# A decoder layer on one core: row maxima written straight into the queries' rows, and a shorter planned distance between attention and output projection

## The chip, the cores and the metric

The kernel runs on one core of a Trainium2 chip. The metric is device time in microseconds (us) of one execution. Engine names are those of the profile: PE is TensorE (PEld its weight loads), DVE VectorE, ACT ScalarE, POOL GpSimd, SP SyncE. SP computes nothing; it issues most DMA transfers, in the order of its program, and a transfer that has to wait for a semaphore holds up everything behind it on SP.

## What is computed

The input x has 16 batches of 128 positions and 1024 channels, and there is a context of the same shape. Cut to what matters here:

```python
# attention: groups of 128 rows are independent; 32 query heads, 8 key heads, head size 32
q, k = rope(x_ln @ Wq), rope(x_ln @ Wk); v = x_ln @ Wv
scores = q @ k.T / sqrt(32), causal
x = x + softmax(scores) @ v @ Wo
# autocorrelation with the context: correlations per channel by Fourier transform,
# the 9 largest delays per channel, softmax over them, weighted sum of delayed values
x = x + autocorrelation(layernorm(x), context)
# four mixed streams: 24 logits per position; a 4x4 matrix by 50 Sinkhorn iterations
# mixes the streams, and one 256x256 branch is added
```

All is float32. The matrix products of the projections run as sums of exact parts (high and low), so that each of them is three products.

## The kernel before, in words

**Two parts.** The first part (lines 182 to 318) projects four batches at a time into rotated queries, keys and values, transforms the context into spectra, and leaves all of it in DRAM (`qd`, `kd`, `vd`, `sd`). Two of the sixteen batches' spectra are left over for the beginning of the second part. The second part (from line 320) takes the batches one by one through attention, output projection, autocorrelation, and mixed streams.

**One batch in the second part** is the generator `batch` (line 775). Its stages, in order:

- `keys` and `queries` (lines 396 and 404) load the keys (`ks`) and, for each half f of the heads (sixteen heads), a tile `qs` of 98 rows. Rows 0 to 95 hold the parts of the queries. Rows 96 and 97 are to hold the negated row maxima, in a high and a low part; the keys' tile has ones there, so that the product of scores (line 447) subtracts the maximum by itself. There are two buffers of `qs`, which is one batch's worth.
- `maxima` (line 412) computes the scores once (line 421), takes the maxima of each row (DVE, line 428) into a tile of [128 positions, 16 heads], transposes it on PE (line 432), and splits the negated result on ACT into `nh` (line 434) and on DVE into `nl` (line 436), both [16 heads, 128 positions]. Then SP writes both to a small DRAM tensor (line 438, two transfers of 8 KB, 32 times two in all) and reads them back as two rows of 2048 values into `qs[96:98]` (line 439, one transfer of 16 KB).
- `attended` (line 441) computes the scores again with the maximum subtracted (line 447), their exponential (ACT, line 451), the causal cut (POOL, line 452), the sums and the values' sums on PE (lines 460 and 464), the division (lines 467 to 476) and its split into `ch` and `cl` (lines 492 and 494). `ch` and `cl` have two buffers each, again one batch's worth; `ch` of the next batch can be written only when the output projection of this one has read it.
- `projected_out` (line 502) is 24 matmuls for each half of the channels (lines 507 to 509), added to `xt` on DVE (line 500). `xt` is loaded just before (line 793, 512 KB).
- Then come the layer norm (`qn`, lines 162 and 169), `delays` (line 528) and `delayed` (line 565). Both call `cross` (line 513), which loads a spectrum of 512 KB into `sv` (line 518; six a batch, two buffers) and multiplies with it on DVE (line 523) and POOL (lines 524 and 525).
- `logits` (line 588) stores `xt` and the normed `z` (lines 590 and 593) and ends in the 24 logits (line 615); `branch` (line 618) ends in an accumulating store that POOL issues (line 657).
- After the last batch of each of three groups (0 to 6, 7 to 12, 13 to 15), `sinkhorn` (line 666) runs 49 iterations of small operations on DVE and POOL, and `mixed` (line 723) mixes the streams of each batch of the group (lines 731 to 766).

**What sets the order.** Each generator yields planned distances in us (`T_...`, lines 36 to 39 and 48), and the loop at line 828 always advances the flow that is due first. A new batch is due every `PERIOD` = 33. That gives the order in which the program is written down, and so the priority of each instruction. The framework then orders every engine's instructions by that priority among those which its own timing model holds to be ready, and inserts the semaphores. So the planned distances are priorities and not times, and an instruction whose buffer is not free is passed by others of lower priority.

**Planned places.** Counted from the due time of its batch, the yields put the first scores of attention at 19.8 and its last sums at 32.9, the output projection at 87.7 and 92.8, the layer norm at 97.9, the store of z at 147.1, the end of the branch at 189.1. The first Sinkhorn blocks of the three groups are due at 387.1, 585.1 and 684.1. The two spectra that are left over are due at 39.7 and 64.2; the first call of `q_late` (line 327, in the output projection of batch 0 at 87.7) would emit what is left of them.

Of the kernel before, what the change touches and what calls it, by code (L numbers as in the profile page):

```python
# [11 lines left out]
FP = mybir.dt.float32  # L12
FR = mybir.dt.float32r
# [7 lines left out]
B, L, D = 16, 128, 1024  # batches, positions, channels  # L21
NK = D // 128  # chunks of 128 channels
HD, NH, NKV = 32, 32, 8  # attention: head size, query heads, key heads
TG = 4  # batches that share one projection
# [3 lines left out]
TOPK = 9  # int(2 * ln(128))  # L28
# [5 lines left out]
# The order of the program: us between batches, and between the parts of one.  # L34
PERIOD = 33
T_S, T_MX, T_M, T_ST, T_PT, T_SUM, T_DIV, T_OUT = 0, 3.29, 13.22, 1.0, 2.56, 54.8, 422239.83, 5.08
T_LN, T_X, T_DEL, T_TOP, T_WT, T_X2, T_DLD = 7.24, 5, 0, 9.35, 3.53, 2.3, 1.0
T_Z, T_ZT, T_LT, T_LOG, T_XP, T_XPT = 15, 2.82, 0.76, 8.03, 14.22, 1.18
SKS, MIXS = [45.0, 257.52, 400.81, 8, 8, 8], [11.22, 56.61, 24.78, 4, 4, 4]
# [8 lines left out]
T_FILL, T_SPEC = 39.7, 24.48  # L48
# [5 lines left out]
# The constant matrices, each [128, 128], in the order in which they lie in the input "mats".  # L54
# [4 lines left out]
def constant_matrices():  # L59
    """Rope tables, causal mask, and the real Fourier matrices of 128 positions.  # L60

    Rows 0..63 of a spectrum are real parts and rows 64..127 imaginary ones. At the even
    frequencies (k / 128) row 0 is frequency 0 and row 64 is frequency 64, both real; the odd ones
    are (k + 1/2) / 128. With a spectrum V of the context and one Q of the other sequence,
    V[re, re] * Q + V[im, im] * [Q im, -Q re] holds the real parts of a cross spectrum and, below
    them, its imaginary parts; at row 0 and 64 of the even frequencies V[im, im] is zero and
    V[re, re] has the real value.

    Frequency 0 adds the same to every correlation of a channel. Neither their order nor their
    softmax depends on it, so that "g" leaves it out, and "f_c" can add to frequency 0 the 128 of  # L70
    the last value by which the even half of the delayed sums lacks half the last value.
    """
    m = {}
    inv = (1.0 / np.float32(500000.0) ** (np.arange(0, HD, 2, dtype=np.float32) / np.float32(HD))).astype(np.float32)
    freqs = (np.arange(L, dtype=np.float32)[:, None] * inv[None]).astype(np.float32)
    m["cos"] = np.repeat(np.cos(freqs).T, 8, 0)
    m["sin"] = np.repeat(np.sin(freqs).T, 8, 0)
    p = np.arange(128)
    m["mask"] = np.where(p[None] > p[:, None], NEG, 0.0)
    m["ident"] = np.eye(128)  # L80
    t, f = np.arange(128)[:, None], np.arange(64)[None]
    sign = (-1.0) ** t
    even = 2 * np.pi * ((t * f) % 128) / 128
    odd = 2 * np.pi * ((t * (2 * f + 1)) % 256) / 256
    im = -np.sin(even)
    im[:, :1] = sign
    m["f_k"] = np.concatenate([np.cos(even), im], 1)
    m["f_c"] = m["f_k"].copy()
    m["f_c"][127, 0] += 128
    m["f_w"] = np.concatenate([np.cos(odd), -np.sin(odd)], 1)  # L90
    # Of the values less the last one.
    m["f_u"] = m["f_w"].copy()
    m["f_u"][127] -= m["f_w"].sum(0)
    g = np.concatenate([np.cos(even), -np.sin(even)], 1).T * 2 / 128
    g[0], g[64] = 0, sign[:, 0] / 128
    m["g"] = g
    ge = np.concatenate([np.cos(even), np.sin(even)], 1).T / 128
    ge[0], ge[64] = 1 / 256, sign[:, 0] / 256
    m["ge"] = ge
    m["go"] = np.concatenate([np.cos(odd), np.sin(odd)], 1).T / 128  # L100
    # Row 32 s + i to column i.
    m["sel"] = (p[:, None] % 32 == p[None]) * 1.0
    return np.ascontiguousarray(np.stack([m[k] for k in FIRST + SECOND], 1).astype(np.float32))


def constant_tokens():
    """Of row 4 t + j, one in column t."""
    return np.repeat(np.eye(32, dtype=np.float32), 4, 0)
# [3 lines left out]
def tile_decoder(ctx: ExitStack, tc, x, cx, wqkv, wo, wlog, base, gate, wb, mats, toks, zero, eye4, out):  # L112
# [3 lines left out]

    SPQ = (SP, ACT)[SQ]
# [6 lines left out]
    # What the first part leaves to the second: rotated queries and keys in two exact parts each,  # L124
    # values, and the context's spectra (even re, even im, odd re, odd im; each twice, below each other).
# [5 lines left out]
    def rsqrt(v, eps):  # L131
        """1 / sqrt(v + eps), with a Newton step behind the tables."""
# [13 lines left out]
    def layernorm(o, i):  # L146
        """Into o; the variance and the factor too."""
        st = small.tile([128, 2, 6], FP, name="st")
        for n in range(2):
            DVE.bn_stats(st[:, n, :], i[:, n * 512 : (n + 1) * 512])  # L150
        mv = small.tile([128, 2], FP, name="mv")
        DVE.bn_aggr(mv, st)
        r = rsqrt(mv[:, 1:2], LN_EPS)
        DVE.tensor_scalar(o, i, mv[:, 0:1], r, ALU.subtract, ALU.mult)
        return mv[:, 1:2], r

    def layernorm_act(o, i, sums, norm):
        """The same on ScalarE, of the sums of two halves."""
# [13 lines left out]
    def over(a, n):  # L172
        """[128, m] -> [128, m, n]"""
        return a.unsqueeze(2).to_broadcast([128, a.shape[1], n])

    def repeat(a, n):
        """[128, m] -> [128, n, m]"""
        return a.unsqueeze(1).to_broadcast([128, n, a.shape[1]])

# [1 line left out]
    # The last spectra fill the beginning of the second part: what they need lies to the right.  # L181
# [3 lines left out]
    with ExitStack() as att:  # L185
# [12 lines left out]
        def weights(j, n):  # L198
            """A block of 256 columns, half of its rows."""
# [39 lines left out]
        def rotated(xh, xl, col, d):  # L239
            """Two chunks of features, of the first and the second halves of eight heads."""  # L240
# [38 lines left out]
        def tokens(g):  # L279
            """Begun before the projections of the group before it are done."""  # L280
# [14 lines left out]
        # Keys, values, then queries.  # L295
# [31 lines left out]
    def q_late():  # L327
        """What the first batch needs behind the last spectra."""
# [36 lines left out]
    # The ninth largest, and no others.  # L365
# [15 lines left out]
    # sigmoid(gate), and (1 - sigmoid(gate)) on the diagonal.  # L381
# [12 lines left out]
    max_d = [[dram.tile([2, 16, 128], FP, name=f"mx{b}_{f}") for f in range(2)] for b in range(B)]  # L394
# [17 lines left out]
    def maxima(b, ks, qs, f):  # L412
        """Of the masked scores of sixteen heads, negated, in two parts into the rows 96 and 97."""
# [19 lines left out]
        nh = q2.tile([16, 128], FR, name="nh")  # L433
        ACT.activation(nh, tp, AF.Copy, scale=-1.0)
        nl = q2.tile([16, 128], FR, name="nl")
        DVE.scalar_tensor_tensor(nl, tp, -1.0, nh.bitcast(FP), ALU.mult, ALU.subtract)
        for i, o in enumerate((nh, nl)):
            SP.dma_start(out=max_d[b][f][i], in_=o.bitcast(FP))
        SP.dma_start(out=qs[96:98, :].bitcast(FP), in_=max_d[b][f].rearrange("i h t -> i (h t)"))

    def attended(b, ks, qs, v, f):
        """Sums over the values of the keys of sixteen heads, and the sums of the weights."""
# [22 lines left out]
        # The reciprocal of the sums, which lie on the rows of the values already.  # L465
# [4 lines left out]
        # A Newton step behind the tables.  # L470
# [26 lines left out]
    def added(xt, n, ps, sums, sign=1.0):  # L497
        """The half n of xt, and its sum."""
# [14 lines left out]
    def cross(b, i, of, m, cols):  # L513
        """Cross spectrum of the context with `of`, [128 positions, 512 channels]."""
# [13 lines left out]
    def delays(b, qn, cols):  # L528
        """Weights of the delays of 512 channels, zero but for the largest."""
# [7 lines left out]
        # The nine largest of each channel become -BIG in `kept`.  # L537
# [27 lines left out]
    def delayed(b, xt, cols, kept, sums):  # L565
        """out[l] = sum of w[tau] v[min(l + tau, 127)]"""
# [21 lines left out]
    def logits(b, xt, lg, sums):  # L588
# [5 lines left out]
        # The mean of z ** 2.  # L594
# [23 lines left out]
    def branch(b, xt, z, lg):  # L618
        # Softmax of the two sets of four.
# [46 lines left out]
    def sinkhorn(Z, n, gi):  # L666
        """exp(Z + u + v) of the last iteration, [128, n, 4, 4]; Z is of that shape too.

        The first iteration runs in logarithms, less the maximum. Behind it every sum over a row or
        a column is within 1/16 and 4 for any Z: the other direction was normalised just before, so  # L670
        that it holds an element of 1/4 at least, divided by a sum of 4 at most. REFRESH iterations
        then scale exp(Z + u + v) itself, and u and v follow from the products of their sums. What
        exp underflows to zero would grow by 16 ** (2 * REFRESH) at most until logarithms take over
        again: to less than 1e-21.
        """
# [3 lines left out]
        # Negated: u, then v.  # L679
# [43 lines left out]
    def mixed(bs, lg):  # L723
        """The mixed streams of some batches, in parts."""
# [10 lines left out]
        # Row (t, j) of 32 positions to row (t, i).  # L735
# [39 lines left out]
    def batch(b):  # L775
        """In parts; each yields the time until the next, as the order of the program has it."""
# [104 lines left out]
```

## Time and profile before

| | |
|---|---|
| times of three runs, us | 1389.58 (the median), 1391.62, 1378.53 |
| span of the profiled execution, first to last instruction, us | 1391.9 |
| its busy time, share of the span: PE, DVE, POOL, ACT | 81%, 63%, 48%, 42% |
| granted TensorE clock, mean of the profile | 0.891 |
| first part of the program | until about 400 us |
| first and last scores of attention (line 447), us | 430.9 and 1104.4 |
| first and last addition of the output projection (line 500), us | 459.9 and 1136.8 |
| last branch (line 657), us | 1223.1 |
| streams mixed (line 761), us | 1228.7 to 1383.0 |

The profiled execution's own time lies in its span of 1391.9 us, which is 0.3 us above the longest of the three runs and 2.3 us above their median. Lines of the profile name an instruction by its line in the kernel, its engine, and what it writes and reads (`qs<-mx` reads the DRAM tensor of the maxima into `qs`). In the lists of waits, the columns are the total idle time in us, how often, and the longest. "SPq" is SP's queue of transfers: such a line says what SP waited for before it could issue.

### The profile page before, as it was taken

Reading aid. Unit: us, or ns where it says so; the run is one execution under the profiler, and the core shown is the slowest. Engines: PE = TensorE matmul, PEld = TensorE weight load, DVE = VectorE, ACT = ScalarE, POOL = GpSimd, SP = SyncE. Lnnn points to the kernel's source line nnn. Section 1 sums busy time; section 2 is a strip of 40 time slices with the busy share of each in tenths; the row PEclk is TensorE's granted clock in tenths of the full one; section 3 lists DMA queues with packets and bytes.
Section 4 is the critical chain, followed back from the end, with each engine's and each line's share of the span. In section 5 each row is a group of like instructions: output and inputs, shape, how many; then the busy total and the mean of one; then the engine's idle time right before and its main releaser. Section 6 shows DMA issues by size and latency. Waiting matters only on the chain.

```text
span 1391.9 us, 17636 instructions
## 1 busy us (share of the span) xinstructions
PE 1134.1 (81%) x5024; PEld 725.9 (52%) x5024; DVE 874.0 (63%) x2910; ACT 580.5 (42%) x1281; POOL 673.0 (48%) x813
## 2 busy tenths in 40 slices
PE   5999969989847999999999998999998976452232
PEld 3888748758623555645565555645564553231121
DVE  5463332321123466977788778968897999986840
ACT  3331221221223355557565666556555755321010
POOL 0353313223413365565566656676766766643332
PEclk9999989989956999999999999999999987655555
DMA  6662864765898444576556664476455444365265
GB/s 227 213 215 84 229 204 123 229 196 137 245 271 250 123 129 140 156 200 166 152 161 170 194 180 135 131 183 156 145 158 153 123 119 115 87 121 106 49 121 76
DMA packets 141824, 221.78 MB, mean 159 GB/s; under 512 B 23264, under 2 KB 86112, under 8 KB 141664
## 3 DMA queue, kind: packets, MB, share of 16 engines
q1 hardware_dynamic: 127936, 199.99, 49.1%
q0 software_dynamic: 10752, 16.78, 8.4%
q10 hardware_dynamic: 3040, 3.90, 0.9%
q8 instruction: 39, 0.64, 0.2%
q14 instruction: 57, 0.47, 0.1%
HBM read 129.93 MB, written 90.83 MB: 159 GB/s over the span
## 4 chain that ended last, share of the span: by engine, by line
PE 40%; DVE 27%; DMA 16%; issue 6%; ACT 4%; SPq 4%; POOL 3%; POOLq 0%; DVEq 0%; ACTq 0%
PE mm L249 4%; PE mm L247 4%; PE mm L248 4%; PE sm L460 4%; PE av L464 3%; PE ps L516 3%; DMA sv<-sd 3%; DMA out<-mx 2%; DVE mx L428 2%; PE o L507 2%; DVE kept L542 2%; DMA sd<-F 2%; PE ps L227 2%; PE o L508 2%; DVE P L523 2%
## 5 line engine op out<-in xcount | busy, mean ns | idle before, releaser
L524 POOL TENSOR_TENSOR s<-s,sv 128x512 f32<-128x512 f32 x96 | 125.2, 1305 | 64.6 <-ACT s L521 47.3
L753 PE MATMUL ps<-mz,hm 128*128 128x256 f32 x128 | 59.4, 622 | 97.5 <-POOL hm L745 71.9
L525 POOL TENSOR_TENSOR P<-P,s 128x512 f32<-128x512 f32 x96 | 125.9, 1313 | 13.3 <-DVE P L523 11.6
L247 PE MATMUL mm<-xh,wh 128*128 128x512 f32 x320 | 131.2, 412 | 0.0
L248 PE MATMUL mm<-xl,wh 128*128 128x512 f32 x320 | 126.6, 396 | 0.2 <-DVE xl L216 0.2
L249 PE MATMUL mm<-xh,wl 128*128 128x512 f32 x320 | 125.5, 392 | 0.0
L257 POOL TENSOR_TENSOR ra<-ra,rb 128x512 f32<-128x512 f32 x40 | 50.4, 1279 | 155.3 <-DVE rb L256 155.2
L507 PE MATMUL o<-woh,ch 128*128 128x512 f32 x256 | 108.9, 425 | 8.3 <-DVE xt L500 6.1
L452 POOL TENSOR_SCALAR_AFFINE_SELECT pt<-pt 128x512 f32<-128x512 f32 x128 | 83.7, 668 | 64.7 <-ACT pt L451 63.0
L508 PE MATMUL o<-woh,cl 128*128 128x512 f32 x256 | 106.8, 417 | 4.7 <-POOL cl L494 4.7
L421 PE MATMUL sc<-ks,qs 96*128 96x128 f32 x512 | 98.2, 323 | 10.1 <-DMA qs<-qd 10.1
L228 ACT COPY F<-ps 128x512 f32<-128x512 f32 x64 | 36.5, 585 | 158.5 <-DMA sd<-F 85.5
L509 PE MATMUL o<-wol,ch 128*128 128x512 f32 x256 | 101.9, 398 | 0.0
L428 DVE TENSOR_REDUCE mx<-sc 128x4 f32<-128x512 f32 x128 | 86.4, 680 | 23.7 <-PE sc L421 23.7
L421 PEld LDWEIGHTS sc<-ks,qs 96*128 96x128 f32 x512 | 82.4, 204 | 33.0 <-issue 26.6
L753 PEld LDWEIGHTS ps<-mz,hm 128*128 128x128 f32 x128 | 36.0, 305 | 120.7 <-POOL hm L745 82.0
L523 DVE TENSOR_TENSOR P<-sv,ps 128x512 f32<-128x512 f32 x96 | 64.8, 675 | 52.6 <-ACT s L521 38.1
L227 PE MATMUL ps<-raw,am 128*128 128x512 f32 x128 | 71.1, 681 | 30.6 <-ACT F L228 25.7
L451 ACT ACTIVATE pt<-sc 128x512 f32<-128x512 f32 x128 | 73.7, 598 | 31.5 <-PE sc L447 30.5
L460 PE MATMUL sm<-pt,ones 128*32 128x512 f32 x256 | 79.7, 617 | 1.9 <-POOL pt L452 1.9
L520 ACT COPY s<-ps 64x512 f32<-64x512 f32 x96 | 56.0, 583 | 55.9 <-PE ps L516 40.2
L516 PE MATMUL ps<-wT,bm 128*128 128x512 f32 x128 | 70.8, 638 | 9.3 <-ACT wT L571 8.9
(171 smaller groups left out, 2852.3 us busy)
## 6 DMA issues: line engine op xcount, KB each, us to landing
sv<-sd SPq DMA_DIRECT2D x96, 512.0 KB
qs<-qd SPq DMA_DIRECT2D x96, 256.0 KB
sd<-F SPq DMA_DIRECT2D x80, 256.0 KB
xt<-in_x SPq DMA_DIRECT2D x32, 512.0 KB
out<-mx POOLq DMA_DIRECT2D x32, 512.0 KB, 5.9
sd<-F SPq DMA_DIRECT2D x48, 252.0 KB
raw<-in_cx SPq DMA_DIRECT2D x16, 512.0 KB
qd<-hi SPq DMA_DIRECT2D x32, 256.0 KB
```

What stands on the lines that cost most here:

```text
L247: PE.matmul(ps, lhsT=wh[:, k, c], rhs=h, start=k == 0, stop=False)
L248: PE.matmul(ps, lhsT=wh[:, k, c], rhs=r, start=False, stop=False)
L249: PE.matmul(ps, lhsT=wl[:, k, c], rhs=h, start=False, stop=k == NK - 1)
L421: PE.matmul(sc[:, j, :], lhsT=qs[0:96, h * 128 : (h + 1) * 128], rhs=ks[0:96, g * 128 : (g + 1) * 128], start=False, stop=j == 3,)
L428: DVE.tensor_reduce(mx[:, 4 * s : 4 * s + 4], sc, AX.X, ALU.max)
L460: PE.matmul(sm[32 * s : 32 * s + 32, :], lhsT=ones, rhs=pt, start=True, stop=True)
L507: PE.matmul(ps, lhsT=h, rhs=woh[:, k, cols], start=k == 0, stop=False)
L508: PE.matmul(ps, lhsT=r, rhs=woh[:, k, cols], start=False, stop=False)
L509: PE.matmul(ps, lhsT=h, rhs=wol[:, k, cols], start=False, stop=k == NK - 1)
L516: PE.matmul(ps, lhsT=M[m], rhs=of, start=True, stop=True)
L524: POOL.tensor_mul(s, s, v[:, 1, :])
L525: POOL.tensor_add(P, P, s)
```

## The change

The maxima go directly from a tile to the queries' rows. `nh` and `nl` become the two halves of one tile `nm`, and for each part one transfer of 8 KB writes sixteen pieces of 512 bytes behind each other into one row of `qs` (row 96 for the high part, row 97 for the low). The DRAM tensor, and the transfer that read it back, are gone. `MAXQ` is SP, so that the queue stays the same.

The planned distances change too. `T_SUM`, between attention and output projection, goes from 54.8 to 13.96; `T_MX`, between the maxima and their transpose, from 3.29 to 4.95 (twice a batch); `T_LN` from 7.24 to 8.24; `T_X2` from 2.3 to 2.82 (twice a batch); the distance between mixed batches of the last group from 24.78 to 25.82; and the distance between the two left-over spectra from 24.48 to 32.17. With these the same counting puts attention's first scores at 23.1, its last sums at 36.2, the output projection at 50.2 and 55.3, the layer norm at 60.4, the store of z at 111.6, the end of the branch at 153.7; the first Sinkhorn blocks are due at 351.7, 549.7 and 648.7. The first call of `q_late` now comes at 50.2, before the second left-over spectrum would be due at 71.9, and emits it. Comments were taken out as well, which changes no instruction.

```diff
-T_S, T_MX, T_M, T_ST, T_PT, T_SUM, T_DIV, T_OUT = 0, 3.29, 13.22, 1.0, 2.56, 54.8, 422239.83, 5.08
-T_LN, T_X, T_DEL, T_TOP, T_WT, T_X2, T_DLD = 7.24, 5, 0, 9.35, 3.53, 2.3, 1.0
+T_S, T_MX, T_M, T_ST, T_PT, T_SUM, T_DIV, T_OUT = 0, 4.95, 13.22, 1.0, 2.56, 13.96, 422239.83, 5.08
+T_LN, T_X, T_DEL, T_TOP, T_WT, T_X2, T_DLD = 8.24, 5, 0, 9.35, 3.53, 2.82, 1.0
-SKS, MIXS = [45.0, 257.52, 400.81, 8, 8, 8], [11.22, 56.61, 24.78, 4, 4, 4]
+SKS, MIXS = [45.0, 257.52, 400.81, 8, 8, 8], [11.22, 56.61, 25.82, 4, 4, 4]
-T_FILL, T_SPEC = 39.7, 24.48
+T_FILL, T_SPEC = 39.7, 32.17
...
+    MAXQ = SP
...
-    max_d = [[dram.tile([2, 16, 128], FP, name=f"mx{b}_{f}") for f in range(2)] for b in range(B)]
...
-        nh = q2.tile([16, 128], FR, name="nh")
-        ACT.activation(nh, tp, AF.Copy, scale=-1.0)
-        nl = q2.tile([16, 128], FR, name="nl")
-        DVE.scalar_tensor_tensor(nl, tp, -1.0, nh.bitcast(FP), ALU.mult, ALU.subtract)
-        for i, o in enumerate((nh, nl)):
-            SP.dma_start(out=max_d[b][f][i], in_=o.bitcast(FP))
-        SP.dma_start(out=qs[96:98, :].bitcast(FP), in_=max_d[b][f].rearrange("i h t -> i (h t)"))
+        nm = q2.tile([16, 2, 128], FR, name="nm")
+        ACT.activation(nm[:, 0], tp, AF.Copy, scale=-1.0)
+        DVE.scalar_tensor_tensor(nm[:, 1], tp, -1.0, nm[:, 0].bitcast(FP), ALU.mult, ALU.subtract)
+        for i in range(2):
+            MAXQ.dma_start(
+                out=qs[96 + i : 97 + i, :].bitcast(FP).rearrange("i (h t) -> i h t", h=16), in_=nm[:, i].bitcast(FP)
+            )
```

## The prediction

> **What bounds the kernel now.** I read the busy times by stretch first, then the waits of the engines and of SP's queue, and last the timeline of one batch in the steady middle.
>
> In the busy times by stretch, the columns are the stretch, its length, each engine's busy time with its number of instructions, the granted TensorE clock, the DMA share and GB/s.
>
> ```profile
> 700.00:800.00 100.00, 95.48 (x479) 57.63 (x476) 81.48 (x257) 61.38 (x138) 63.26 (x63) 1.00 0.61 172
> 1000.00:1100.00 100.00, 93.78 (x435) 53.29 (x434) 83.97 (x288) 60.98 (x139) 69.66 (x98) 0.98 0.56 149
> 1100.00:1150.00 50.00, 40.11 (x174) 22.96 (x172) 47.79 (x181) 29.53 (x72) 37.02 (x53) 0.90 0.42 127
> 1150.00:1225.00 75.00, 42.03 (x136) 21.89 (x134) 72.58 (x315) 32.55 (x82) 46.64 (x79) 0.68 0.36 94
> 1225.00:1392.00 167.00, 55.89 (x120) 33.34 (x120) 90.80 (x464) 21.32 (x50) 53.92 (x106) 0.54 0.55 98
> ```
>
> Three stages are to be seen. Up to 1100 PE is busy for 94 to 95 us of 100, at nearly the full clock, with VectorE at 81 to 84. From 1100 to 1225, where the last batches run out, VectorE is the bound (47.79 of 50, 72.58 of 75). From 1225 on nothing is near full: that is the last Sinkhorn iterations and the mixing of sixteen batches. The last stage hangs on the last logits and on its own transfers (ACT waits 82.8 us for `out<-mx` there), and the change touches neither. So a gain has to come from the middle, or from the running out.
>
> The waits of the engines, then those of SP's queue (total, times, longest):
>
> ```profile
> POOL s L524 <- DMA sv<-sd: 14.9, 8, 4.3
> PE sc L447 <- DMA qs<-mx: 7.4, 6, 3.3
> DVE P L523 <- DMA sv<-sd: 4.9, 6, 1.9
> ```
>
> ```profile
> SPq L518 <- DVE P L523: 144.7, 57, 8.4
> SPq L439 <- DMA mx<-nl: 62.8, 30, 4.1
> SPq L439 <- DMA mx<-nh: 6.6, 3, 3.5
> ```
>
> The transfer that is to go stops SP for 62.8 + 6.6 = 69.4 us in all, but PE itself has waited for the maxima for only 7.4 us. What stands behind the stopped SP are mostly the loads of spectra into `sv`, and for these the engines wait 14.9 + 4.9 = 19.8 us.
>
> One batch of the middle in the timeline (start, duration, engine, line):
>
> ```profile
> 722.94 0.33 SPq L593 DMA_DIRECT2D zd<-z  x1
> 723.19 0.27 PE L432 MATMUL sc<-ident,mx 128*16 128x128 f32 x1
> 723.37 0.44 SPq L793 DMA_DIRECT2D xt<-in_x  x1
> 723.90 0.68 SPq L438 DMA_DIRECT2D mx<-nh  x1
> 724.63 0.41 SPq L438 DMA_DIRECT2D mx<-nl  x1
> 728.78 0.23 SPq L439 DMA_DIRECT2D qs<-mx  x1
> 729.12 0.38 SPq L518 DMA_DIRECT2D sv<-sd  x1
> 730.79 0.47 PE L447 MATMUL sc<-qs,ks 98*128 98x512 f32 x1 [0.29 <-DMA qs<-mx]
> ```
>
> From the transpose of the maxima to the scores that need them pass 7.6 us. The chain of waits of the same stretch splits what follows the transfer's issue:
>
> ```profile
> 724.63 4.08 DMA mx<-nl
> 728.78 1.87 DMA qs<-mx
> ```
>
> Each of the two hops is a bare transfer of 8 or 16 KB. The first takes 4.08 us because a store of `z` and a load of `xt`, 512 KB each, were issued just before it. Where nothing large stands in front, SP can issue the read 1.35 us after the last write (1093.47 and 1094.82 in the timeline). PE meanwhile has other work and loses only 0.29 us here.
>
> **The transfers, costed.** Per part one hop goes: a read of `qs<-mx` of 1.87 us. Two writes remain, now into `qs`.
>
> - *PE's wait.* The six waits are 1.2 us long on average, less than the hop that goes, so I take all 7.4 us away. The longest (3.3 us) may leave some behind; that is at most 3.3 - 1.87 = 1.4 us.
> - *SP's stop.* With no read there is no wait between write and read, and what is queued behind it (a load of `sv`, a load of `qs`, or the stores of `xt` and `z`) can be issued up to 4.1 us sooner. The waits of engines for `sv` are 19.8 us. But line 518 stops SP by itself for 144.7 us because the buffer is still being read, so many of these loads gain nothing. Ends: 0 and 19.8. The two kinds of stop say that neither end is near, so I take the middle, 9.9.
> - *SP's issues.* 96 become 64; at 0.23 us for each of 32 reads that is 7.4 us of SP, which is idle for long. Cost and gain nothing; if SP were full, 7.4 us more of gain.
> - *ACT and VectorE.* Lines 434 and 436 stay at 0.27 us each, 32 times; only their tile changes. Nothing.
> - *The new transfer.* The trace shows no write of sixteen pieces into one row of a tile. Nearest are the write of the same sixteen pieces to DRAM (1.35 us up to 4.08 us behind large loads) and the read into the same two rows (1.87 us). If it behaves as the first, the sum stands. If it needs both times, 4.08 + 1.87, nothing is gained. I take the first: same pieces, same queue, same neighbours.
>
> A rule that bears on it is in the Trainium skill, "DMA: Bandwidth & Descriptors", section "Why a DMA increments its semaphore by 16 and not by 1": the outermost dimension of both sides decides over how many DMA engines a transfer is spread. By it the removed read of two rows used two engines and the new writes, with sixteen rows, use all sixteen, and so end only when the slowest of sixteen has worked off the loads in front. That speaks against more than the hop's gain, and agrees with the 4.08 us above. Against the change stands also the table "Rules for kernel authors" of that page, which wants small transfers coalesced; by it two writes into `qs` in place of one read should cost, and the sum would be nearer to zero than mine.
>
> **The order, costed.** The output projection and all behind it is written down 87.7 - 50.2 = 37.5 planned us earlier in its batch (35.5 from the logits on). Moved with it past the attention of later batches are: 48 matmuls and two additions; on SP the loads of `xt`, six of `sv`, and the stores of `xt` and `z`; on POOL twelve multiplications and the accumulating store. The planned period is 33, the real one 43.9 (line 500's first addition at 673.6, 717.5, 761.6).
>
> Does the real order follow the old plan? By the plan the projection comes 54.8 planned us behind the last sums, that is behind the attention of two more batches. In the timeline, attention's second half is multiplied out at 707.25 (line 476), the first half's projection is running already at 703.84 and the second half is added at 717.5 and 724.4. The reason is the two buffers of `ch`: the next batch's attention can't write before this projection has read, so the framework lets the projection pass. The new plan (14 planned us, some 19 real ones at 43.9 / 33) writes down what is done already. I therefore cost it at nothing in the likeliest case; what covers it is this buffer limit.
>
> Its ends are wide. For a gain: if all that was moved were really done 37.5 × 43.9 / 33 = 50 us earlier while attention keeps its pace, the running out of 1100 to 1225 would lose up to 50 us. For a loss: attention is the stage that lives on few buffers (`qs`, `ch`), and until now it had the right of way whenever a buffer was free. Now the layer norm of the batch before is written ahead of it: 1144 + 187 ns on ACT (line 162) and 968 ns on VectorE (line 169), 2.3 us. If this stands in attention's way at each of the two halves, it is 4.6 us × 15 batches = 69 us; at one half, 35 us. In the waits, whoever waits for attention then is PE at line 447 and 460, and behind it SP's load of the next `qs` (line 409), which waits for line 447.
>
> The earlier spectrum of batch 15 (50.2 instead of 64.2) comes while PE is not full (80.70 busy of the 100 us from 400 on); nothing. The Sinkhorn blocks move with their batches, by 35.5, and keep their place against the last branch; the wider `T_MX`, `T_LN` and `T_X2` are in the 37.5 and 35.5.
>
> **Sum.** 7.4 + 9.9 = 17.3 us less. Against the profiled execution, 1391.9 - 17.3 = 1374.6. Its span is 2.3 us above the median of the runs shown, 1389.58, from which I count: 1372.3 us.
>
> **Rivals.**
>
> 1. *Likeliest: the hop goes, the order stays as it is.* 1372, with 1358 to 1388: from 7.4 + 19.8 + 4 for a shorter wait at `qs` loads to 1.4 only.
> 2. *The running out shortens as well.* Half of the 50 us on top: 1347; for it speaks that VectorE, at 95% and more from 1100 to 1225, had idle time before (18% at 700 to 800) that earlier work could use. Against it, the real order already has the projection near.
> 3. *The transfers were hidden anyway.* PE lost only 7.4 us to them; if the new write takes the place of both hops, or the `sv` loads wait for their buffers, 1390 within 8.
> 4. *Slower: attention loses its right of way.* Place: PE's line 447 of the second half, behind layer norm and spectra of the batch before. Price: 35 to 69 us, less the 17: 1407 to 1441. It decides as soon as the delay per batch is over 17.3 / 15 = 1.2 us. For it speaks that the loop of `qs` (load, maxima, transpose, transfer, scores) fills the whole period of 43.9, so that each delay in it is paid. Against it, the freed hop gives 1.87 us a part back to the same loop.
>
> **How the numbers follow.** About 1% is what a measurement of this kernel can tell from no change (1375.7 to 1403.5). Case 1 has 0.42, of which 0.28 below 1375.7 and 0.14 within 1%. Case 2 has 0.16, all faster. Case 3 has 0.10, all within 1%. Case 4 has 0.32, of which 0.02 within 1%. Faster 0.44, same 0.26, slower 0.30. The range that leaves out no more than 2 in 10 cuts off the lower part of case 2 and the upper of case 4: 1340 to 1425.
>
> **What would show it.** Right: no line 439 in SP's waits on `mx`; the wait of PE's line 447 for the transfer into `qs` near zero; POOL's wait at line 524 for `sv` below 14.9; first additions of line 500 still some 44 us or a little less apart, and the last logits (1213 now) some 17 us earlier. For case 2 the stretch from the last scores (1104.4) to the last branch (1223.1) would be clearly below 119 us. For case 4 the additions would be 46 us apart or more, with new waits at line 447, or SP waiting longer than 84.2 us at line 409. A span that changes in the last 169 us, behind the last branch, would make all of this wrong.

## The result, and the profile after

The changed kernel takes 1397.43 us (median of 20 runs), the kernel before 1392.81 in as many runs beside it. The ratio is 1.0041, with a 95% interval from 1.0025 to 1.0058. That is slower by 0.25 to 0.58%: measurable here, but within the 1% that the prediction called no change. The forecast was 17.3 us less; it became 4.6 us more.

The profiled execution has a span of 1393.4 us. Its busy times by stretch, cut as those of before (the last stretch is a microsecond longer):

```profile
700.00:800.00 100.00, 93.69 (x424) 54.86 (x425) 75.57 (x236) 58.01 (x129) 58.07 (x60) 0.97 0.58 157
1000.00:1100.00 100.00, 92.77 (x447) 56.35 (x446) 89.66 (x321) 62.65 (x146) 70.20 (x99) 0.98 0.54 150
1100.00:1150.00 50.00, 40.22 (x189) 21.58 (x187) 46.47 (x179) 32.94 (x77) 37.78 (x54) 1.00 0.42 116
1150.00:1225.00 75.00, 40.22 (x132) 20.69 (x133) 72.57 (x290) 31.11 (x78) 44.40 (x73) 0.68 0.36 98
1225.00:1393.00 168.00, 58.25 (x130) 34.89 (x128) 93.70 (x489) 23.21 (x54) 56.19 (x111) 0.55 0.55 98
```

The same three stages with the same bounds. Read the first row by its counts: PE is nearly as busy as before (93.69 against 95.48), but it did 424 matmuls there and not 479, and VectorE 236 instructions and not 257. So a stretch can be "full" and yet get less done. A stretch of 100 us also depends on which stages happen to fall into it: in the second row the changed kernel has more matmuls than before. Over 500 us of the middle, first before and then after, it has 68 matmuls and 20 VectorE instructions less:

```profile
560.00:1060.00 500.00, 471.17 (x2252) 275.04 (x2250) 408.47 (x1348) 305.58 (x689) 321.92 (x375) 0.99 0.60 164
```

```profile
560.00:1060.00 500.00, 464.40 (x2184) 273.77 (x2184) 405.49 (x1328) 298.08 (x670) 307.78 (x367) 0.98 0.57 157
```

So the time went in the steady middle.

The waits of the engines for transfers, then those of SP's queue:

```profile
POOL s L524 <- DMA sv<-sd: 13.4, 6, 5.2
DVE P L523 <- DMA sv<-sd: 6.8, 4, 2.4
```

```profile
SPq L518 <- DVE P L523: 163.4, 67, 6.2
SPq L409 <- PE sc L447: 110.1, 29, 9.0
SPq L437 <- ACT nm L434: 59.9, 16, 11.8
```

PE's wait of 7.4 us for the maxima is gone, and with it SP's stops on a landed transfer of maxima (69.4 us). The waits for `sv` are 20.2 us (13.4 + 6.8) where they were 19.8. And SP now stops longer for buffers that are still being read: line 518 went from 144.7 to 163.4, line 409 from 84.2 to 110.1.

The distances between the logits of the batches (line 615), from the traces of both kernels, place the loss (us):

| | before | after |
|---|---|---|
| first logits | 556.8 | 546.0 |
| a batch, batches 2 to 6 | 43.7 | 46.1 |
| logits of batch 6 | 820.9 | 822.2 |
| a batch, batches 6 to 12 | 47.3 | 47.4 |
| last logits | 1213.0 | 1217.0 |
| from there to the end of the span | 178.9 | 176.4 |

The shorter plan does bring the first logits 10.8 us earlier. Batches 2 to 6 give some 9.5 of it back (four times 2.4), and from there on nothing is gained.

### The profile page after: what moved, and what is told of

The parts are those of the page before. It is cut to its first block, busy times and chain, and to the rows that moved or that the text cites. A ratio compares the mean times of both kernels' runs of the same rounds, so it can differ in the third digit from the quotient of the medians.

```text
span 1393.4 us, 17602 instructions
## 1 busy us (share of the span) xinstructions
PE 1125.4 (81%) x5024; PEld 725.1 (52%) x5024; DVE 885.4 (64%) x2910; ACT 583.1 (42%) x1281; POOL 669.7 (48%) x813
## 4 chain that ended last, share of the span: by engine, by line
PE 28%; DVE 23%; DMA 9%; issue 7%; ACT 6%; SPq 4%; POOL 4%; POOLq 0%; DVEq 0%; ACTq 0%
PE sm L460 3%; PE ps L516 3%; PE av L464 3%; PE o L507 2%; PE o L508 2%; DMA sv<-sd 2%; PE o L509 2%; DMA sv<-in_wo 2%; PE sc L447 2%; DMA out<-mx 2%; DVE mx L428 2%; DMA sd<-F 2%; DVE P L523 2%; DVE kept L542 2%; DVE xt L500 1%
## 5 line engine op out<-in xcount | busy, mean ns | idle before, releaser
L507 PE MATMUL o<-woh,ch 128*128 128x512 f32 x256 | 108.1, 422 | 12.7 <-DVE xt L500 12.7
L516 PE MATMUL ps<-wT,bm 128*128 128x512 f32 x128 | 71.8, 646 | 17.4 <-ACT wT L571 13.4
L262 POOL TENSOR_TENSOR lo<-ra,hi 128x512 fp32r<-128x512 f32 x40 | 52.1, 1312 | 57.5 <-ACT hi L260 57.5
L255 DVE TENSOR_TENSOR ra<-mm,am 128x512 f32<-128x512 f32 x40 | 25.8, 683 | 76.7 <-PE mm L250 66.7
```

The source lines that it names most:

```text
L507: PE.matmul(ps, lhsT=h, rhs=woh[:, k, cols], start=k == 0, stop=False)
L516: PE.matmul(ps, lhsT=M[m], rhs=of, start=True, stop=True)
```

## The experiments

Each kernel was timed against the kernel before, beside it on the same chip, and each ratio is given with its 95% interval. "The way through DRAM" is that of before, "direct" is that of the changed kernel. A ratio of 1.001 is 1.4 us.

### The two halves of the change alone

`e1_direct` has only the direct transfers:

```diff
-        nh = q2.tile([16, 128], FR, name="nh")
...
-        SP.dma_start(out=qs[96:98, :].bitcast(FP), in_=max_d[b][f].rearrange("i h t -> i (h t)"))
+        nm = q2.tile([16, 2, 128], FR, name="nm")
...
+            SP.dma_start(
+                out=qs[96 + i : 97 + i, :].bitcast(FP).rearrange("i (h t) -> i h t", h=16), in_=nm[:, i].bitcast(FP)
+            )
```

> The direct transfers alone, with the planned distances of before. Theory A (the hop gives a little back and the earlier projection takes it away): 5 to 17 us faster, ratio 0.988 to 0.996. Rival B (the hop was hidden, and what is measured comes from the order alone): ratio 0.997 to 1.003. Rival C (the new transfer of sixteen pieces costs more than the hop that went): ratio 1.003 or more.

Measured: 0.9968 (0.9945 to 0.9991), about 4.5 us less; that lies between the ranges of theory A and rival B. Its waits for `sv`, and the stops at line 518:

```profile
POOL s L524 <- DMA sv<-sd: 14.5, 9, 2.1
DVE P L523 <- DMA sv<-sd: 3.9, 5, 1.1
```

```profile
SPq L518 <- DVE P L523: 185.2, 71, 8.4
```

No PE wait for the maxima is left in its list, which is the 7.4 us. But the `sv` waits are 18.4 where they were 19.8. SP waits 40.5 us longer at line 518 for the buffer (144.7 to 185.2): a good part of what it no longer loses in front of line 439 it loses here.

`e2_order` has only the planned distances, with the way through DRAM:

```diff
-... = 0, 3.29, 13.22, 1.0, 2.56, 54.8, 422239.83, 5.08
-... = 7.24, 5, 0, 9.35, 3.53, 2.3, 1.0
+... = 0, 4.95, 13.22, 1.0, 2.56, 13.96, 422239.83, 5.08
+... = 8.24, 5, 0, 9.35, 3.53, 2.82, 1.0
-SKS, MIXS = [45.0, 257.52, 400.81, 8, 8, 8], [11.22, 56.61, 24.78, 4, 4, 4]
-T_FILL, T_SPEC = 39.7, 24.48
+SKS, MIXS = [45.0, 257.52, 400.81, 8, 8, 8], [11.22, 56.61, 25.82, 4, 4, 4]
+T_FILL, T_SPEC = 39.7, 32.17
```

> The planned distances of the changed kernel alone, with the way through DRAM as before. Theory A: 10 to 22 us slower, ratio 1.007 to 1.016, with more time between the additions of the output projection in the middle and an earlier first batch. Rival B: ratio 1.002 to 1.006, the whole of the measured change. Rival C: ratio 0.99 to 1.000, since then the order does not cost.

Measured: 1.0091 (1.0061 to 1.012). The distances that the prediction had costed at nothing are the loss.

### Which distance

`e3_tsum` is the kernel before with the one large distance shortened:

```diff
-T_S, T_MX, T_M, T_ST, T_PT, T_SUM, T_DIV, T_OUT = 0, 3.29, 13.22, 1.0, 2.56, 54.8, 422239.83, 5.08
+T_S, T_MX, T_M, T_ST, T_PT, T_SUM, T_DIV, T_OUT = 0, 3.29, 13.22, 1.0, 2.56, 13.96, 422239.83, 5.08
```

> Only the distance between attention and output projection goes from 54.8 to 13.96; all else as before. If the nearer projection is what costs (theory A), as slow as the run with all planned distances, within 0.3%. If it is one of the small distances that rides along (4.95, 8.24, 2.82, 32.17), ratio 0.997 to 1.002 here.

Measured: 1.0000 (0.9972 to 1.0028). The 41 planned us cost and gain nothing in sum. In before, after, `e1_direct` and `e3_tsum` alike the first addition of the projection (line 500) follows 6 to 12 us, mostly 8 to 10, behind the division of attention's second half (line 476): the projection was right behind its attention all along.

`e4_hop3` asks what a hop is worth from the other side; it adds one more transfer from DRAM to DRAM:

```diff
+    max_e = [[dram.tile([2, 16, 128], FP, name=f"me{b}_{f}") for f in range(2)] for b in range(B)]
-        SP.dma_start(out=qs[96:98, :].bitcast(FP), in_=max_d[b][f].rearrange("i h t -> i (h t)"))
+        SP.dma_start(out=max_e[b][f], in_=max_d[b][f])
+        SP.dma_start(out=qs[96:98, :].bitcast(FP), in_=max_e[b][f].rearrange("i h t -> i (h t)"))
```

> One suspected cost doubled: the maxima go through two DRAM tensors one after the other, one more transfer and one more wait of SP per part; planned distances as before. Theory A: one hop is worth 5 to 17 us, so 5 to 20 us slower, ratio 1.004 to 1.015. Rival B (hidden): ratio 0.997 to 1.003. Rival C says nothing of this.

Measured: 1.024 (1.0207 to 1.0274), some 33 us. The scores' line (449 here) now waits for the longer way, on PE and in its weight loads:

```profile
PE sc L449 <- DMA qs<-me: 21.1, 11, 4.0
PEld sc L449 <- DMA qs<-me: 18.4, 9, 4.1
```

That is beyond every range that was expected. A hop more costs seven times what a hop less brings: PE now waits for the maxima, where it had waited for 7.4 us before. PE's own instructions came in another order too, so how the 33 us split between latency and order stays open.

`e5_tsum_x2` adds to `e3_tsum` the second suspect, `T_X2`, which each half of `delayed` passes once:

```diff
-T_LN, T_X, T_DEL, T_TOP, T_WT, T_X2, T_DLD = 7.24, 5, 0, 9.35, 3.53, 2.3, 1.0
+T_LN, T_X, T_DEL, T_TOP, T_WT, T_X2, T_DLD = 7.24, 5, 0, 9.35, 3.53, 2.82, 1.0
```

> Way through DRAM; T_SUM 13.96 and, of the small distances, only T_X2 2.82 (between the two cross spectra of the delayed sums). Theory A after the first runs: T_SUM alone costs nothing, so the loss of the order sits in a small distance, and T_X2 is the one that rearranges most rows. Then ratio 1.005 to 1.012 here. Rival D (no single distance: each new order that the framework makes is a new draw, some per mil better or worse): anything between 0.995 and 1.012, and the run without T_X2 not complementary to this one.

Measured: 1.0056 (1.0029 to 1.0083). Half a planned microsecond costs 0.56%.

`e6_order_x223` is `e2_order` with that one number put back:

```diff
-T_LN, T_X, T_DEL, T_TOP, T_WT, T_X2, T_DLD = 8.24, 5, 0, 9.35, 3.53, 2.82, 1.0
+T_LN, T_X, T_DEL, T_TOP, T_WT, T_X2, T_DLD = 8.24, 5, 0, 9.35, 3.53, 2.3, 1.0
```

> Way through DRAM; all planned distances of the changed kernel, but T_X2 back at 2.3. Theory A: the loss goes, ratio 0.997 to 1.003. If T_MX or T_LN carries the loss: ratio 1.006 to 1.012. Rival D: anything in between, unrelated to the run with T_X2.

Measured: 0.9967 (0.9941 to 0.9993). All other distances of the change together are a gain of 0.33%; `T_X2` alone turns it into a loss of 0.91%.

### The hop, with the order held

`e7_direct_tsum` is `e1_direct` with the edit of `e3_tsum`; `e8_after_x223` is the changed kernel with the edit of `e6_order_x223`.

> Direct transfers and T_SUM 13.96, all other distances as before. If the parts add up: 0.9968 times 1.0000, so ratio 0.994 to 0.999. Rival D: not additive, 1.000 or more.

Measured: 0.9995 (0.997 to 1.002), where the way through DRAM had given 1.0000. This is the fairest price of the hop: in these two, the order of instructions is the same on VectorE, ScalarE and POOL, and PE's differs in one place only (a product of scores has moved ahead of some sums of attention). It is not distinguishable from nothing. In this order the way through DRAM had little left to give, either: in `e3_tsum` PE's line 447 waits for the maxima for 1.8 us in all. And SP's stop moves again, with the order held: line 518 waits for 169.4 us in `e3_tsum` and for 198.4 in `e7_direct_tsum`.

> The changed kernel with T_X2 back at 2.3. Theory A: the direct transfers' gain is left, ratio 0.994 to 1.000. Rival D: no relation, as likely above 1.003.

Measured: 1.0001 (0.9975 to 1.0027). With this one number put back the changed kernel is level with the kernel before; without it, it was 1.0041.

### Why half a planned microsecond

`z`, the start of `logits`, is due in its batch at `T_TOP + 2 (T_WT + T_X2 + T_X) + T_DLD` behind the search of the largest delays in the second half of `delays` (lines 534 to 562). The next batch's search is due 33 later than this one's. Before, the difference is 9.35 + 2 × (3.53 + 2.3 + 5) + 1.0 - 33 = -0.99: `z` is written down ahead of that search. With 2.82 it is +0.05: behind it. `T_SUM` and `T_LN` drop out of it. In the changed plan `T_X2` swaps other pairs, too: counted over the planned places of all batches (the Sinkhorn blocks left out), twelve more pairs of stages of different batches. Two kernels therefore test this crossing with other numbers than `T_X2`; counted in the same way, they swap `z` with this search and no other pair.

`e9_order_swap_back` is `e2_order` with `z` due 0.6 earlier, and what follows it where it was (difference -0.55):

```diff
-T_LN, T_X, T_DEL, T_TOP, T_WT, T_X2, T_DLD = 8.24, 5, 0, 9.35, 3.53, 2.82, 1.0
-T_Z, T_ZT, T_LT, T_LOG, T_XP, T_XPT = 15, 2.82, 0.76, 8.03, 14.22, 1.18
+T_LN, T_X, T_DEL, T_TOP, T_WT, T_X2, T_DLD = 8.24, 5, 0, 9.35, 3.53, 2.82, 0.4
+T_Z, T_ZT, T_LT, T_LOG, T_XP, T_XPT = 15.6, 2.82, 0.76, 8.03, 14.22, 1.18
```

> Way through DRAM, all planned distances of the changed kernel with T_X2 2.82, but the start of the second layer norm (z) alone is put 0.6 planned us earlier (T_DLD 0.4, T_Z 15.6), so that it stands ahead of the second half of the next batch's delays again, as it did with T_X2 2.3. Theory A': the loss of T_X2 is this one crossing; ratio 0.995 to 1.000, as in the run with T_X2 2.3. If it is the cross spectra's own place: ratio 1.006 to 1.012, as with all distances. Rival D (each order a new draw): anything between.

Measured: 0.9965 (0.9946 to 0.9984), the lowest ratio of all. It agrees with the 0.9967 of `e6_order_x223` for a plain reason: by the traces the two start the same instructions in the same order on PE, ScalarE and POOL, and on VectorE but for two small Sinkhorn operations (lines 707 and 711). The same holds of `e8_after_x223` and `e11_after_swap_back` below. So as long as `z` is ahead of the search, the twelve other pairs change nothing that runs.

`e10_swap_alone` is `e6_order_x223` with `z` due 1.04 later (difference +0.05), by `T_DLD` 2.04 and `T_Z` 13.96.

> The converse: way through DRAM, all planned distances of the changed kernel but T_X2 2.3, and the start of z alone 1.04 planned us later (T_DLD 2.04, T_Z 13.96), which puts it behind the second half of the next batch's delays. Theory A': ratio 1.005 to 1.012. If the crossing is not it: ratio 0.995 to 1.000.

Measured: 1.0034 (1.0018 to 1.005), so +0.67% from the crossing alone. That is short of the 1.005 that was expected at least, and doesn't reach the 1.0091 of `e2_order`; what the rest of `T_X2` does once `z` is behind is not isolated. What is paid for is not the one pair by itself: PE's order in this kernel differs from that of `e6_order_x223` in about a hundred places, which all follow from it.

`e11_after_swap_back` is the changed kernel with the edit of `e9_order_swap_back`.

> The changed kernel, direct transfers included, with z alone 0.6 planned us earlier. Theory A': as the changed kernel with T_X2 2.3, which came to 1.0001; ratio 0.996 to 1.002, and below the changed kernel's own 1.0041. Otherwise 1.003 to 1.006.

Measured: 0.9992 (0.9973 to 1.001).

Without `e4_hop3`, with its longer way, and `e12_direct_early4` below, the kernels now fall into two groups. Eight have `z` ahead of the search (before, `e1_direct`, `e3_tsum`, `e6_order_x223` to `e9_order_swap_back`, `e11_after_swap_back`): 0.9965 to 1.0001. Four have it behind (the changed kernel, `e2_order`, `e5_tsum_x2`, `e10_swap_alone`): 1.0034 to 1.0091. The traces place the difference where the table above has it: by the logits, a batch takes 43.2 to 44.8 us in batches 2 to 6 of the eight and 45.6 to 46.6 in the four, while batches 6 to 12 don't tell them apart (46.5 to 47.5, and 46.5 to 47.7).

Which wait makes up this difference is not shown. Two waits for ScalarE's results between 640 and 820 look as if they did; first `e9_order_swap_back` (the same in `e11_after_swap_back`), then the changed kernel:

```profile
DVE P L523 <- ACT s L521: 3.5, 4, 0.9
POOL pt L452 <- ACT pt L451: 8.0, 5, 1.6
```

```profile
DVE P L523 <- ACT s L521: 14.8, 9, 2.9
POOL pt L452 <- ACT pt L451: 15.9, 8, 3.7
```

They are 11.3 and 7.9 us longer in the slower kernel. But the kernel before, with 43.7 us a batch, has as much of the one and more of the other:

```profile
DVE P L523 <- ACT s L521: 24.0, 14, 2.9
POOL pt L452 <- ACT pt L451: 15.6, 10, 3.0
```

It is the same with the eight exponentials of a batch (line 451): they take 13.5 us in `e11_after_swap_back` (batches 6 to 9, from the start of the first to the end of the last) and 15.1 to 16.9 in the changed kernel (batches 5 to 8), but 16.0 to 16.6 in the same batches of before, too.

One wait of PE does keep the groups apart in this stretch. All four kernels with `z` behind stop at line 578, at the end of `delayed`, for POOL's sum of the cross spectra, and none of the eight does. In the changed kernel:

```profile
PEld ps L578 <- POOL P L525: 4.2, 2, 2.4
PE ps L578 <- POOL P L525: 3.5, 2, 2.1
```

On PE it is 1.8 to 4.5 us in the four, less than the loss, and between 560 and 1060 the kernel before has one such stop as well (2.1 us). So what loses the time is the order; the way from it to the 2.4 us a batch stays open.

And the counts again, over 560 to 1060, of `e9_order_swap_back` and of `e2_order`:

```profile
560.00:1060.00 500.00, 470.77 (x2290) 275.08 (x2289) 420.97 (x1364) 311.80 (x698) 327.89 (x384) 1.00 0.62 165
```

```profile
560.00:1060.00 500.00, 468.57 (x2205) 274.74 (x2204) 401.06 (x1323) 298.76 (x670) 309.92 (x360) 0.98 0.58 159
```

PE is as busy in the one as in the other and does 85 matmuls more in the one; VectorE's busy time shows the difference openly (420.97 against 401.06 us).

### A try for a better version

`e12_direct_early4` is `e1_direct` with the short distance for the first four batches only, to keep the early start and leave the middle as it was:

```diff
-        yield T_SUM
+        yield T_SUM if b >= 4 else 13.96
```

> Direct transfers and the distances of before, with T_SUM 13.96 for the first four batches only and 54.8 from then on. If the earlier start of the output projection (11 us at the first logits of the changed kernel) is worth keeping and the old order holds the pace of the middle: ratio 0.988 to 0.995. If the early gain is given back in the middle whatever the order: ratio 0.996 to 1.000, as with the direct transfers alone.

Measured: 1.0114 (1.0083 to 1.0145), a miss. Where the two distances meet, the logits of batches 3 and 4 are 77.4 us apart, and the first addition of batch 4 comes 38 us behind its attention, not 9. PE is full in that gap:

```profile
640.00:680.00 40.00, 39.49 (x198) 25.17 (x197) 21.03 (x57) 17.93 (x39) 14.59 (x15) 1.00 0.56 146
```

In these 40 us PE does 71 matmuls of the output projection and none of `delays` (line 534); in the same stretch of `e1_direct` they are 48 and 16. VectorE and POOL, which in this part work mostly on what the spectra's matmuls leave, are busy for 21.03 and 14.59 of 40. The uniform distance of 54.8 in `e1_direct` opens no such gap; the mixed one does.

The gap shows one thing more. From batch 4 on the planned distance is 54.8 as in the kernel before, yet the first addition stays 26 to 43 us behind its attention (11.8 in batch 5) and not 8 to 10. So the two buffers of `ch` don't hold the projection close to its attention by themselves; in this kernel they leave it room for nearly a batch.

## Why the prediction was wrong, point by point

The step that failed is "The order, costed": "I therefore cost it at nothing in the likeliest case". The order was the larger term, and of the other sign: `e2_order` alone is 0.91% or 12.7 us slower. The transfers were the other part of the miss: 17.3 us were forecast for them, and `e1_direct` has 4.5. The two halves add up to 8.2 us more, where the whole change has 4.6.

- *PE's wait: 7.4 us taken away.* The wait is gone in `e1_direct` and in the changed kernel, as forecast. The 4.5 us of `e1_direct` (1.3 to 7.7 by its interval) leave room for nothing more than this term; that they are this term is not shown, as its order of instructions differs from before.
- *SP's stop: the middle between 0 and 19.8, 9.9.* Wrong; the lower end was the value. `e1_direct` waits 18.4 us for `sv` against 19.8. The prediction named the reason, line 518's wait for the buffer, and then took half all the same: with the read gone, that wait grew by 40.5 us (29.0 from `e3_tsum` to `e7_direct_tsum`).
- *SP's issues: 7.4 us less.* Wrong in sign; no run shows what it is worth. See the last section.
- *The new transfer behaves as the write to DRAM.* PE never waits for it at line 447 in `e1_direct` or in the changed kernel, so nothing there speaks against it; how long it takes to land was not measured. The rule of the Trainium skill, "DMA: Bandwidth & Descriptors", table "Rules for kernel authors", that small transfers should be coalesced, pointed to a smaller gain than the sum; the gain was smaller, but that PE had waited for only 7.4 us explains it without that rule, and no run here separates the two.
- *The real order has the projection right behind its attention.* Right, as the traces show, and `e3_tsum` (1.0000) agrees: the large part of the shift is worth nothing, as costed. The reason that was given, the two buffers of `ch`, is not enough: `e12_direct_early4` has the same buffers and the projection 26 to 43 us behind.
- *"The wider `T_MX`, `T_LN` and `T_X2` are in the 37.5 and 35.5."* This is where the step broke. They were counted as part of a common shift, and their effect is relative: `T_X2` moves `z` 1.04 past its neighbours, and carries it across the next batch's search, from 0.99 ahead to 0.05 behind. Everything needed to find it stood in the code. Undone by `T_X2` or by `z` alone, which comes to the same order, it gives back 1.24 and 1.26% with the way through DRAM, 0.40 and 0.49% in the changed kernel; made alone, it costs 0.67%, and by `T_X2` on top of `T_SUM` 0.56%. The sign is the same every time, the size is not, and why it costs what it does is open.
- *The rivals.* Case 3, the transfers hidden anyway, 1390 within 8, holds the time, and what it says of the hop is borne out by 0.9995 against 1.0000 in one order. Case 4 had the right sign and the wrong mechanism. It wanted the layer norm of `qn` written ahead of the next attention, which `e3_tsum` does at no cost; what costs is the stage of `z`, a batch further on, written behind the next batch's search. The price was 6 to 18 us (0.40 to 1.26%), not 35 to 69. Its signs came all the same: the first additions are 46.8 us apart from batch 2 to 12 (45.3 before), and SP's wait at line 409 went to 110.1, beyond the 84.2 that were named. But that wait is 104.9 in `e11_after_swap_back` too, so it tells little. Case 2: the last scores (1110.3) and the last branch (1227.5) are 117.2 us apart against 118.7; not it.
- *What would show it.* "No line 439", "near zero at line 447": right. "`sv` below 14.9" at line 524: 13.4, but VectorE has 6.8 where it had 4.9, so that the sum is no smaller. "The last logits some 17 us earlier": 4.0 later.

What the hop is worth stays undecided below half a per cent. Direct less DRAM, in five pairs with the same planned distances, is -0.32 (`e1_direct`), -0.05 (`e7_direct_tsum`), +0.34 (`e8_after_x223`), +0.27 (`e11_after_swap_back`) and -0.50% (the changed kernel against `e2_order`). In all but the second the framework also writes another order of PE's instructions, so four of the five carry an order's effect as well. The third and the fourth are one comparison made twice, since their kernels have the same orders, and in each of them both ways were timed beside each other; there the direct way is slower, and why is not explained.

The best versions are `e9_order_swap_back` (0.9965) and `e6_order_x223` (0.9967), which are all but one program, and `e1_direct` (0.9968). They are level within their intervals and faster than both kernels. The first two keep the way through DRAM.

## What to carry to other kernels

When priorities change, don't sum the shift: write down which pairs of stages of neighbouring batches change places, and treat each as a term of unknown sign until a run has it alone. Here one pair was worth 0.4 to 1.3%, and twelve others nothing while that one was held. A transfer that its reader waited for 7 us in all brought no more than that when it went; the queue that it freed stopped at the next buffer instead. Under a full engine compare counts of instructions, not busy shares. And before a longer wait is called the loss, look for it in a kernel that hasn't lost.

## What the runs showed of the hardware

The direct write costs SP more to issue than the write to DRAM. These are the rows of `qs<-nm` of the changed kernel (ns, least, median, most):

```profile
L437 SPq DMA_DIRECT2D qs<-nm x64: 502/509/2052, 423.2 to 1096.3; - x64
```

and these those of before:

```profile
L438 SPq DMA_DIRECT2D mx<-nh x32: 302/330/1155, 422.2 to 1092.5; - x32
L438 SPq DMA_DIRECT2D mx<-nl x32: 312/370/679, 423.0 to 1093.5; - x32
L439 SPq DMA_DIRECT2D qs<-mx x32: 229/233/248, 427.1 to 1094.8; - x32
```

For the same 8 KB in sixteen pieces it takes 0.51 us where the write to DRAM takes 0.33 or 0.37. So by the medians two issues now hold SP for 1.02 us a part, and the three of before did for 0.93. Fewer transfers did not mean less time of the queue.
